# A convolution and a Laplace layer: the pole transform over 128 couples of opposite frequencies, the conjugate rows of the residues exchanged inside the matmul, and the table pieces spaced

## The chip, the cores and the metric

The kernel runs on one NeuronCore of a Trainium2 chip. The metric is the device time of one execution in microseconds (us). The engines are TensorE (PE, with its weight loads shown as PEld), VectorE (DVE), ScalarE (ACT), GpSimd (POOL) and SyncE (SP), which here only issues transfers. Each engine works through its own instructions in order.

## The reference, cut to what matters

Two layers, each added to its input after a group normalization. The first is a circular 3x3 convolution. The second multiplies the 2-D Fourier transform of the image by rational functions of the frequency, given by poles and residues. All is float32, with 16 images of 16 channels of 256 x 256.

```python
def reference(x, w, ty, tx, pole1, pole2, residue):
    x = x + conv3x3_circular(group_norm(x), w)                  # layer 0
    v = group_norm(x)                                           # layer 1
    alpha = fft2(v)
    omega1 = 2j*pi*fftfreq(Ny, dty); omega2 = 2j*pi*fftfreq(Nx, dtx)
    A  = 1.0 / (omega1[:, None, None, None] - pole1[None])      # [256, i, o, 4]
    Bm = 1.0 / (omega2[:, None, None, None] - pole2[None])
    S  = einsum('ikpq,oikp,xikq->oxik', residue, A, Bm)
    r1 = einsum('biox,oxik->bkox', alpha, S)                    # transfer function
    C  = einsum('biox,oikp->bikpx', alpha, A)                   # projections on the poles
    D  = einsum('bikpx,xikq->bikpq', C, Bm)
    r2 = einsum('bikpq,ikpq->bkpq', D, residue)
    x1 = ifft2(r1).real
    x2 = ...  # sum over p, q of r2 * exp(pole1 * ty) * exp(pole2 * tx), real part
    return x + x1 + x2 / (Nx * Ny)
```

For the projections the kernel does not transform the images with A and Bm at every frequency. It transforms A and Bm themselves along the frequency axis, once, into tables of functions of the position: that is the pole transform. For each side there are 16 x 16 x 4 = 1024 complex poles. 1/(i*w - p) at the frequencies w and -w has numerators and denominators in common, which the change uses.

## The kernel before

There are four stages. In the first the convolution runs image by image, in 24 steps an image, and between its steps small pieces of set-up work are issued: statistics of the next image, and generators that build tables for the later stages. The second takes the transforms of the images and the projections, the third sums and mixes with the residues, the fourth transforms back and writes the result. The set-up generators and the loop of the first stage:

```python
    def omega(o, k, d):
        nc.vector.tensor_scalar(o, k, d, 2.0 * PI, ALU.mult, ALU.mult)

    def make_hat(side):                      # pole transform, side 0 = y, 1 = x
        nc.sync.dma_start(out=hatT, in_=a[f"hatT{side}"])
        kcol = sw.tile([P, 2], FP, name="s_kcol", tag="s_kcol")
        nc.sync.dma_start(out=kcol, in_=a["kcol"])
        omega(kcol, kcol, rd[:, side : side + 1])
        n = C * C * 4
        to = ((tabE[:, 1:], tabO[:, :C]), (hB[:, 0], hB[:, 1]))[side]
        for half in range(2):
            pb = sw.tile([P, n // 2, 2], FP, name="s_pb", tag="s_pb")
            nc.sync.dma_start(
                out=pb,
                in_=a[f"pole{side + 1}"][half * 512 : half * 512 + 512].partition_broadcast(P),
            )
            yield
            re = [sw.tile([P, n // 2], FP, name="s_re", tag=f"s_re{h}") for h in range(2)]
            im = [sw.tile([P, n // 2], FP, name="s_im", tag=f"s_im{h}") for h in range(2)]
            dens = [sw.tile([P, n // 2], FP, name="s_den", tag=f"s_den{h}") for h in range(2)]
            pr, pi = pb[:, :, 0], pb[:, :, 1]
            for h in range(2):
                k = kcol[:, h : h + 1]
                nc.scalar.activation(im[h], pi, AF.Identity, bias=k, scale=-1.0)
                nc.scalar.activation(dens[h], pi, AF.Square, bias=k, scale=-1.0)
                if h == 0:
                    nc.gpsimd.tensor_tensor(re[1], pr, pr, ALU.mult)
                nc.gpsimd.tensor_tensor(dens[h], dens[h], re[1], ALU.add)
                yield
            for h in range(2):
                w, r, den = im[h], re[h], dens[h]
                nc.vector.reciprocal(den, den)
                yield

                nc.gpsimd.tensor_tensor(r, pr, den, ALU.mult)
                nc.vector.scalar_tensor_tensor(w, w, -1.0, den, ALU.mult, ALU.mult)
                yield
            yield
            for eo in range(2):
                hv = to[eo].rearrange("p i (m r) -> p i m r", r=2)[:, 8 * half : 8 * half + 8]
                for ri in range(2):
                    ps = psu.tile([P, 512], FP, name="ps_setup", tag="ps_setup")
                    for h in range(2):

                        parts = (((2, re), (1, im)), ((0, im), (1, re)))[ri]
                        for j, (at, src) in enumerate(parts):
                            nc.tensor.matmul(
                                ps,
                                lhsT=hatT[:, h, at, eo],
                                rhs=src[h],
                                start=h == 0 and j == 0,
                                stop=h == 1 and j == 1,
                            )
                        yield
                    nc.scalar.copy(hv[:, :, :, ri], ps.rearrange("p (i m) -> p i m", i=8))

    def make_coef():


    # ... make_coef, make_exps (the exponentials' tables): not touched ...

    def make_c():                            # the residues' matrices
        # ... loads, poles' parts, rc[:, st]: residues, st = 1 the conjugate ...
        for k0 in range(0, C, 2):
            # ... den, num on POOL; yield
            nc.vector.reciprocal(den, den)
            # ... w on POOL: 128 rows x (s = 2, i = 4, m = 8) columns for each of odd, i0 + ii
            yield
            nc.gpsimd.tensor_tensor(num, num, den, ALU.mult)
            yield
            yield
            c4 = sw.tile([P, 4, N], FP, name="s_c", tag="s_pb")
            for i0 in range(0, 4, 2):
                c = c4[:, i0 : i0 + 2]
                ps = psu.tile([P, 2, N], FP, name="ps_setup", tag="ps_setup")
                for ii in range(2):
                    for odd in range(2):
                        nc.tensor.matmul(
                            ps[64 * odd : 64 * odd + 64, ii],
                            lhsT=w[:, odd, i0 + ii].rearrange("p s i m -> p (s i m)"),
                            rhs=num[:, odd],
                            start=True,
                            stop=True,
                        )
                yield
                nc.scalar.copy(c, ps)

                for odd in range(2):
                    rows = slice(64 * odd + 32, 64 * odd + 64)
                    o = c[rows].rearrange("p i (h n) -> p i h n", h=2)
                    s = ps[rows].rearrange("p i (h n) -> p i h n", h=2)
                    for h in range(2):
                        copy = (nc.scalar.copy, nc.vector.tensor_copy)[odd]
                        copy(o[:, :, h, 1:], s[:, :, 1 - h, 1:])
                yield
            nc.sync.dma_start(out=cD[:, :, k0 // 2], in_=c4)

    # ... the loop over the steps of the convolution
    tables = (
        (2, 0, chain(make_hat(0), make_hat(1), make_c())),
        (5, 1, chain(make_exps(0), make_exps(1), make_coef())),
    )
    for g in range(24 * B + 3):
        conv(g)                              # 16 matmuls of 32 x 32 x 512, evictions on ACT
        # ... loads of images, statistics of the next image
        for every, first, gen in tables:
            if g % every == first:
                next(gen, None)              # one piece: up to the generator's next yield
```

A `yield` ends a piece, so one piece of the first chain is issued after every second step of the convolution, and one of the second chain after every fifth. `ps_setup` is a pool with one PSUM buffer, shared by all pieces. In `conv(g)` the tiles have 32 rows and 32 columns, so that sixteen matmuls can stand in the array beside each other; an accumulation takes six steps.

The constants of the pole transform (`hatT`) hold cosines and sines of all 256 frequencies, in two halves of 128, each folded into even and odd positions (`eo`).

Of the kernel before, what the change touches and what calls it, by code (L numbers as in the profile page):

```python
# [9 lines left out]
FP = mybir.dt.float32  # L10
AF = mybir.ActivationFunctionType
ALU = mybir.AluOpType
# [5 lines left out]
C = 16  # L18
N = 256
P = 128  # L20
PI = float(np.pi)
# [3 lines left out]
def conv_then_laplace_kernel(ctx: ExitStack, tc: tile.TileContext, a: dict, out: bass.AP):  # L25
# [15 lines left out]
    nc = tc.nc  # L41
# [3 lines left out]
    dp = ctx.enter_context(tc.tile_pool(name="scratch", bufs=1, space=DRAM))  # L45
# [6 lines left out]
    cols = const("cols", [P, 24])  # L52
# [7 lines left out]
    aD = dp.tile([P, 2 * C, N * B], FP, name="aD", tag="aD")  # L60
    yD = dp.tile([P, 2 * C, 4, 4, 16 * B], FP, name="yD", tag="yD")
    cD = dp.tile([P, 4, 8, N], FP, name="cD", tag="cD")
    eD = [dp.tile([n, P, C, 2, P], FP, name=f"eD{n}", tag=f"eD{n}") for n in (2, 1)]


    def omega(o, k, d):
        nc.vector.tensor_scalar(o, k, d, 2.0 * PI, ALU.mult, ALU.mult)
# [4 lines left out]
    rd = cp.tile([P, 2], FP, name="rd", tag="rd")  # L72
# [24 lines left out]
    p1 = ExitStack()  # L97
    wp = p1.enter_context(tc.tile_pool(name="conv_w", bufs=1))
# [5 lines left out]
    sw = p1.enter_context(tc.tile_pool(name="setup", bufs=1))  # L104
# [241 lines left out]

    def make_hat(side):

        hatT = wp.tile([P, 2, 3, 2, P], FP, name="hatT", tag="hatT")
        nc.sync.dma_start(out=hatT, in_=a[f"hatT{side}"])
        kcol = sw.tile([P, 2], FP, name="s_kcol", tag="s_kcol")
        nc.sync.dma_start(out=kcol, in_=a["kcol"])
        omega(kcol, kcol, rd[:, side : side + 1])
        n = C * C * 4
        to = ((tabE[:, 1:], tabO[:, :C]), (hB[:, 0], hB[:, 1]))[side]
        for half in range(2):  # L360
            pb = sw.tile([P, n // 2, 2], FP, name="s_pb", tag="s_pb")
            nc.sync.dma_start(
                out=pb,
                in_=a[f"pole{side + 1}"][half * 512 : half * 512 + 512].partition_broadcast(P),
            )
            yield
            re = [sw.tile([P, n // 2], FP, name="s_re", tag=f"s_re{h}") for h in range(2)]
            im = [sw.tile([P, n // 2], FP, name="s_im", tag=f"s_im{h}") for h in range(2)]
            dens = [sw.tile([P, n // 2], FP, name="s_den", tag=f"s_den{h}") for h in range(2)]
            pr, pi = pb[:, :, 0], pb[:, :, 1]  # L370
            for h in range(2):
                k = kcol[:, h : h + 1]
                nc.scalar.activation(im[h], pi, AF.Identity, bias=k, scale=-1.0)
                nc.scalar.activation(dens[h], pi, AF.Square, bias=k, scale=-1.0)
                if h == 0:
                    nc.gpsimd.tensor_tensor(re[1], pr, pr, ALU.mult)
                nc.gpsimd.tensor_tensor(dens[h], dens[h], re[1], ALU.add)
                yield
            for h in range(2):
                w, r, den = im[h], re[h], dens[h]  # L380
                nc.vector.reciprocal(den, den)
                yield

                nc.gpsimd.tensor_tensor(r, pr, den, ALU.mult)
                nc.vector.scalar_tensor_tensor(w, w, -1.0, den, ALU.mult, ALU.mult)
                yield
            yield
            for eo in range(2):
                hv = to[eo].rearrange("p i (m r) -> p i m r", r=2)[:, 8 * half : 8 * half + 8]
                for ri in range(2):  # L390
                    ps = psu.tile([P, 512], FP, name="ps_setup", tag="ps_setup")
                    for h in range(2):

                        parts = (((2, re), (1, im)), ((0, im), (1, re)))[ri]
                        for j, (at, src) in enumerate(parts):
                            nc.tensor.matmul(
                                ps,
                                lhsT=hatT[:, h, at, eo],
                                rhs=src[h],
                                start=h == 0 and j == 0,  # L400
                                stop=h == 1 and j == 1,
                            )
                        yield
                    nc.scalar.copy(hv[:, :, :, ri], ps.rearrange("p (i m) -> p i m", i=8))

    def make_coef():

# [67 lines left out]
    def make_c():  # L475
# [4 lines left out]
        om = space[:, 0:N]  # L480
# [3 lines left out]
        z = space[:, 2 * N : 2 * N + 64].rearrange("p (j k) -> p j k", j=4)  # L484
# [30 lines left out]
        for k0 in range(0, C, 2):  # L515

            at = k0 // 2 % 2
# [11 lines left out]
            for odd in range(2):  # L529
                for st in range(2):  # L530
# [10 lines left out]
                        ALU.mult,  # L541
                    )
            yield
            nc.gpsimd.tensor_tensor(num, num, den, ALU.mult)
            yield
            yield
            c4 = sw.tile([P, 4, N], FP, name="s_c", tag="s_pb")
            for i0 in range(0, 4, 2):
                c = c4[:, i0 : i0 + 2]
                ps = psu.tile([P, 2, N], FP, name="ps_setup", tag="ps_setup")  # L550
                for ii in range(2):
                    for odd in range(2):
                        nc.tensor.matmul(
                            ps[64 * odd : 64 * odd + 64, ii],
                            lhsT=w[:, odd, i0 + ii].rearrange("p s i m -> p (s i m)"),
                            rhs=num[:, odd],
                            start=True,
                            stop=True,
                        )
                yield  # L560
                nc.scalar.copy(c, ps)

                for odd in range(2):
                    rows = slice(64 * odd + 32, 64 * odd + 64)
                    o = c[rows].rearrange("p i (h n) -> p i h n", h=2)
                    s = ps[rows].rearrange("p i (h n) -> p i h n", h=2)
                    for h in range(2):
                        copy = (nc.scalar.copy, nc.vector.tensor_copy)[odd]
                        copy(o[:, :, h, 1:], s[:, :, 1 - h, 1:])
                yield  # L570
            nc.sync.dma_start(out=cD[:, :, k0 // 2], in_=c4)

    def chain(*gens):
        for gen in gens:
            yield from gen
# [8 lines left out]
    for b in range(1, B):  # L584
        at_step.setdefault(max(0, 24 * b - 40), []).append((b, x_stats(b)))
    going = []
    tables = (
        (2, 0, chain(make_hat(0), make_hat(1), make_c())),
        (5, 1, chain(make_exps(0), make_exps(1), make_coef())),
    )  # L590
    early = v_stats(0, B - 4, lambda: pst.tile([P, 512], FP, name="ps_stat", tag="ps_stat"))
# [633 lines left out]
def _constants():  # L1225
# [23 lines left out]
        [w * tcos.T[ox], w * tsin.T[ox], -w * tsin.T[ox], tcos.T[o], tsin.T[o]], 1  # L1249
    )  # L1250

    th = 2 * np.pi * (np.outer(j, j) % N) / N
    t = np.stack([np.cos(th), np.sin(th)]).reshape(2, 2, P, N)
    t = np.stack([t[..., :P] + t[..., : P - 1 : -1], t[..., :P] - t[..., : P - 1 : -1]], 3) / 2

    t = np.concatenate([t, -t[:1]]).transpose(2, 1, 0, 3, 4)
    c["hatT0"] = t
    lo, hi = t[..., :64], t[..., :63:-1]
    c["hatT1"] = np.concatenate([lo + hi, lo - hi], -1) / 2
    k = (j + P) % N - P  # L1260
    c["kcol"] = k.reshape(2, P).T
    c["kslot"] = np.concatenate([p, -f_sin])[None]
    c["kmask"] = p[:, None] // 8 == np.arange(C)[None]
    cols = np.zeros((P, 24))
# [48 lines left out]
def _laid_out(x, L0_conv_weight, L1_conv_ty, L1_conv_tx, L1_conv_weights_pole1, L1_conv_weights_pole2, L1_conv_weights_residue):  # L1313
# [26 lines left out]
        pairs(np.asarray(z))  # L1340
        for z in (L1_conv_weights_pole1, L1_conv_weights_pole2, L1_conv_weights_residue)
    )
    g["pole1"], g["pole2"] = p1.reshape(-1, 2), p2.reshape(-1, 2)

    g["res_kq"] = np.repeat(rs.transpose(1, 3, 0, 2, 4).reshape(64, C, 4, 2), 2, 0)

# [28 lines left out]
```

## Time and profile before

| | |
|---|---|
| time before | 2893.25 us, median of 3 runs (2887.61 to 2897.32) |
| span of the profiled execution | 2897.0 us |
| busy: PE, PEld, DVE, ACT, POOL | 92%, 68%, 67%, 53%, 35% |
| first stage (convolution and tables) | 0 to 726 us; first convolution matmul at 29.6 us |
| convolution matmuls (L238) | 12288 instructions, 477.4 us busy |
| pole transform matmuls (L396) | 128 instructions, first at 54.8 us, last at 313.9 us |
| residue matmuls (L553) | 128 instructions, first at 340.9 us, last at 552.6 us |
| chain that ended last | begins at 739 us and ends with the kernel |

One float32 matmul of the program shows as two MATMUL instructions in the profile, so 64 transform matmuls give 128 instructions. A row of the groups reads: line, engine, operation, output <- inputs, shape and count; then the busy time of the group and the mean duration of one instruction in ns; then the time that the engine sat idle just before them and which instruction ended it. Ends of matmuls are modelled, so starts are the better mark. "issue" is a gap for which the profile shows no wait.

### The profile page before, as it was taken

The numbers are of one execution on the slowest core, as the hardware profiler recorded it, in microseconds if no ns is written. First come the engines' busy times: TensorE is split into PE (matmuls) and PEld (weight loads), VectorE is DVE, ScalarE is ACT, GpSimd is POOL, SyncE is SP. The second block draws the span as 40 slices with busy tenths as digits, with TensorE's granted clock in tenths as the row PEclk, the third lists the DMA queues.
The fourth block names the chain that finished last, engine by engine and source line by source line (L and its number), as shares of the span: only waits on it lengthen the run. The fifth ranks groups of instructions, "written<-read, shape, count | busy, mean of one in ns | idle before, by whom it ended". The sixth has DMA issues, their size and how long they took to land.

```text
span 2897.0 us, 92787 instructions
## 1 busy us (share of the span) xinstructions
PE 2667.3 (92%) x39536; PEld 1971.8 (68%) x39536; DVE 1940.5 (67%) x3572; ACT 1536.0 (53%) x3098; POOL 1003.5 (35%) x906
## 2 busy tenths in 40 slices
PE   4878878889799999997899999999969999999998
PEld 2333334346577777775688888888868888888887
DVE  7766698886788888887444444444427666766666
ACT  3556677667466666664345555555524444444443
POOL 2232566420233333333211111111135554555553
PEclk9989998899899999998899999999989999999999
DMA  6555667665566666664466666666679999888995
GB/s 257 203 179 187 212 238 256 229 240 192 182 211 211 233 233 224 227 218 169 150 193 191 191 196 193 193 192 191 190 212 312 285 285 288 285 284 285 290 288 188
DMA packets 477335, 650.63 MB, mean 225 GB/s; under 512 B 49065, under 2 KB 458665, under 8 KB 462969
## 3 DMA queue, kind: packets, MB, share of 16 engines
q1 hardware_dynamic: 472920, 635.37, 67.0%
q8 instruction: 312, 5.11, 0.7%
q10 hardware_dynamic: 3408, 7.34, 0.7%
q0 software_dynamic: 592, 1.97, 0.3%
q14 instruction: 103, 0.84, 0.1%
HBM read 365.09 MB, written 279.45 MB: 222 GB/s over the span
## 4 chain that ended last, share of the span: by engine, by line
PE 56%; DMA 9%; DVE 6%; SPq 2%; POOL 1%; issue 1%; ACT 0%; DVEq 0%; ACTq 0%; POOLq 0%
PE ps_mix L967 15%; PE ps_s L909 8%; PE ps_y L678 8%; PE ps_y L686 8%; DMA yk<-yD 4%; PE ps_x L721 4%; PE ps_p L1148 4%; PE ps_f L1157 3%; PE ps_f L1158 3%; DMA out_y<-ol 3%; DVE r L1166 2%; PE psd L706 1%; DVE ol L1168 1%; DVE ol L1169 1%; SPq L1099 1%; DMA yD<-yt 1%
## 5 line engine op out<-in xcount | busy, mean ns | idle before, releaser
L238 PE MATMUL ps_conv<-xt,wc 32*32 32x512 f32 x12288 | 477.4, 641 | 18.0 <-ACT vt L255 11.2
L967 PEld LDWEIGHTS ps_mix<-abd,sg 128*64 128x64 f32 x8192 | 448.5, 138 | 65.5 <-ACT sg L1027 49.8
L967 PE MATMUL ps_mix<-abd,sg 128*64 128x128 f32 x8192 | 479.4, 276 | 13.4 <-ACT yt L1032 13.4
L1112 POOL TENSOR_TENSOR u<-yk 128x512 f32<-128x512 f32 x256 | 342.2, 1366 | 369.8 <-PE ps_p L1148 241.6
L694 ACT ACTIVATE t<-ps_y,vmr 128x384 f32<-128x384 f32 x512 | 297.7, 582 | 168.4 <-PE ps_y L686 157.0
L238 PEld LDWEIGHTS ps_conv<-xt,wc 32*32 32x32 f32 x12288 | 231.8, 106 | 214.8 <-issue 142.1
L1032 DVE COPY yt<-ps_mix 128x512 f32<-128x512 f32 x128 | 88.6, 692 | 363.8 <-PE ps_mix L967 231.8
L678 PE MATMUL ps_y<-tabE,vq 128*128 128x256 f32 x1024 | 313.1, 387 | 13.9 <-DVE vq L667 12.2
L887 POOL TENSOR_TENSOR w<-v,mcol 128x2048 f32<-128x2048 f32 x33 | 119.3, 3614 | 583.8 <-DVE v L884 580.8
L1157 PE MATMUL ps_f<-pt,inv 128*128 128x256 f32 x1024 | 305.8, 380 | 0.0
L686 PE MATMUL ps_y<-tabO,vq 128*128 128x256 f32 x1024 | 305.7, 380 | 0.0
L1158 PE MATMUL ps_f<-hs,ey 128*128 128x256 f32 x1024 | 305.0, 379 | 0.0
L1032 ACT COPY yt<-ps_mix 128x512 f32<-128x512 f32 x384 | 221.6, 587 | 147.2 <-PE ps_mix L967 95.8
L1148 PEld LDWEIGHTS ps_p<-inv,u 128*128 128x128 f32 x2048 | 265.1, 192 | 49.2 <-issue 24.3
L1148 PE MATMUL ps_p<-inv,u 128*128 128x128 f32 x2048 | 278.1, 279 | 12.6 <-POOL u L1115 12.5
L909 PE MATMUL ps_s<-ct,w 64*32 64x256 f32 x8448 | 260.6, 382 | 27.1 <-DMA ct<-cD 27.1
L1161 DVE TENSOR_TENSOR r<-ps_f,q 128x256 f32<-128x256 f32 x256 | 107.2, 419 | 252.1 <-ACT q L1160 252.1
L255 ACT ACTIVATE vt<-ps_conv,xq 128x512 f32<-128x512 f32 x256 | 167.1, 680 | 194.0 <-PE ps_conv L238 193.0
L1027 ACT COPY sg<-ps_s 128x512 f32<-128x512 f32 x248 | 159.9, 646 | 199.7 <-PE ps_s L909 199.5
L678 PEld LDWEIGHTS ps_y<-tabE,vq 128*128 128x128 f32 x1024 | 189.5, 190 | 90.3 <-ACT q L734 50.3
L1160 ACT COPY q<-ps_f 128x256 f32<-128x256 f32 x256 | 95.4, 373 | 290.8 <-PE ps_f L1158 290.8
L909 PEld LDWEIGHTS ps_s<-ct,w 64*32 64x32 f32 x8448 | 158.4, 107 | 92.3 <-POOL abd L1011 27.9
(214 smaller groups left out, 4165.0 us busy)
## 6 DMA issues: line engine op xcount, KB each, us to landing
xt<-in_x SPq DMA_DIRECT2D x32, 2322.0 KB, 9.6
abd<-aD SPq DMA_DIRECT2D x512, 128.0 KB, 3.3
yD<-yt SPq DMA_DIRECT2D x512, 128.0 KB, 2.6
vl<-vD SPq DMA_DIRECT2D x256, 256.0 KB, 3.9
out_y<-ol SPq DMA_DIRECT2D x128, 512.0 KB, 9.8
yk<-yD SPq DMA_DIRECT2D x63, 1024.0 KB, 8.6
s<-vD SPq DMA_DIRECT2D x244, 256.0 KB, 5.9
aD<-spec SPq DMA_DIRECT2D x15, 4096.0 KB, 13.3
```

What stands on the lines that cost most here:

```text
L238: nc.tensor.matmul(acc[r][32 * c : 32 * c + 32], lhsT=ready[b][0][rows, phase, tap], rhs=halves[b][u // 2][rows, q : q + 5 : 4, 2 - tap : ...
L255: nc.scalar.activation(vt[:, r % 2], acc[r], AF.Identity, bias=ready[b][1], **by_sums)
L678: nc.tensor.matmul(ps[:, 0:N], lhsT=vf[:, xo, 0, j], rhs=tabE[:, 0 : i + 2 : i + 1], start=True, stop=False, skip_group_check=True,)
L686: nc.tensor.matmul(ps[:, P : P + N], lhsT=vf[:, xo, 1, j], rhs=tabO[:, i : C + 1 : C - i], start=False, stop=True, skip_group_check=True,)
L694: nc.scalar.activation(t[:, xo, j].rearrange("p l n -> p (l n)"), ps[:, 0:384], AF.Copy, scale=vmr[:, 0, b0 + j, i : i + 1],)
L909: nc.tensor.matmul(ps[odd][32 * iq : 32 * iq + 32, ro], lhsT=w[rows, iq, kk, ro], rhs=ct[rows, iq, kk], start=True, stop=True,)
L967: nc.tensor.matmul(ps[64 * t : 64 * t + 64, j], lhsT=sg[:, f : f + 2].rearrange("p f m -> p (f m)"), rhs=abd[jq][:, :, 2 * t + cc, 2 * jj ...
L1032: (nc.vector.tensor_copy if m == 3 else nc.scalar.copy)(o, src)
L1112: nc.gpsimd.tensor_tensor(u[:, :, j].rearrange("p b (c n) -> p c b n", c=8), in0, in1, o)
L1148: nc.tensor.matmul(ps[:, at], lhsT=u[:, n], rhs=tab, start=True, stop=True)
L1157: nc.tensor.matmul(ps[:, e], lhsT=tab, rhs=pt[:, e], start=True, stop=False)
L1158: nc.tensor.matmul(ps[:, e], lhsT=ey[:, e], rhs=hs, start=False, stop=True)
```

## The change

Three things are changed, all in the set-up generators of the first stage.

The pole transform is taken over 128 couples (w, -w) instead of 256 frequencies. The sum and the difference of 1/(iw - p) and 1/(-iw - p) are rational in w squared: with m = |p|^2, sq = re^2 - im^2 and nb = -2 re im, the common denominator is g = (w^2 + sq)^2 + nb^2, and the four real quantities needed come from re, im, m, sq and nb. These five depend on the pole alone. A new generator, `make_poles`, computes them once for all poles, 16 values in each of 128 partitions, writes them to a scratch tensor in DRAM (`hD`), and `make_hat` loads them spread over all partitions. The couple in partition 0 is made of the frequencies 0 and 128; its values go into `hD` as two further rows (qr, qi) and are loaded over row 0.

For the residues, the conjugate rows (`st` = 1) need the two halves of the frequencies exchanged. Before, copies out of PSUM did that; now the matmul of those rows reads its moving operand with the halves reversed, so the matmuls have 32 columns instead of 64, and only entries 0 and 128 are exchanged by copies.

Further `yield`s are put between the pieces: after the copy out of the setup bank, ahead of the product of `num`, and after the loads.

```diff
+    hD = dp.tile([7, 2, C * C * 4], FP, name="hD", tag="hD")
 ...
+    def make_poles():
+        pz = sw.tile([P, 64, 16], FP, name="s_pz", tag="s_pb")
+        re, im, m, sq, nb, qr, qi, r2, t = (pz[:, j] for j in range(9))
+        nc.sync.dma_start(out=pz[:, 0:2], in_=a["poles"])
+        yield
+        yield
+        # ... thirteen-odd small operations on DVE: m, sq, nb, qr, qi, -im
+        yield
+        nc.sync.dma_start(
+            out=hD.rearrange("c s (p e) -> p (c s) e", e=8),
+            in_=pz[:, 0:7].rearrange("p c (s e) -> p (c s) e", e=8),
+        )
+        yield
+        yield
 ...
     def make_hat(side):
 ...
+        n = C * C * 2
         for half in range(2):
 ...         # the body shown above is replaced
+            pr, npi, m, sq, nb, g, b2 = tiles
+            at = slice(half * n, half * n + n)
+            for j in range(5):
+                nc.sync.dma_start(out=tiles[j], in_=hD[j, side, at].partition_broadcast(P))
+            yield
+            yield
+            if half == 0:
+                omega(om1, om1, rd[:, side : side + 1])
+                nc.vector.tensor_tensor(om2, om1, om1, ALU.mult)
+                # ... hatT[:, 1] is scaled by om1 (1 in row 0)
+            yield
+            nc.scalar.activation(g, sq, AF.Square, bias=om2)
+            nc.scalar.activation(b2, nb, AF.Square)
+            yield
+            nc.gpsimd.tensor_tensor(g, g, b2, ALU.add)
+            yield
+            nc.vector.reciprocal(g, g)
+            yield
+            for z in (pr, npi, nb):
+                nc.gpsimd.tensor_tensor(z, z, g, ALU.mult)
+            yield
+            nc.vector.scalar_tensor_tensor(sq, sq, om2, g, ALU.add, ALU.mult)
+            yield
+            nc.vector.scalar_tensor_tensor(pr, m, om2, pr, ALU.add, ALU.mult)
+            nc.vector.scalar_tensor_tensor(npi, m, om2, npi, ALU.subtract, ALU.mult)
+            for j, z in ((5, sq), (6, nb)):
+                nc.sync.dma_start(out=z[0:1], in_=hD[j, side, at].unsqueeze(0))
+            yield
             yield
             for eo in range(2):
 ...
+                for ri, parts in enumerate(((pr, sq), (npi, nb))):
                     ps = psu.tile([P, 512], FP, name="ps_setup", tag="ps_setup")
+                    for j, src in enumerate(parts):
+                        nc.tensor.matmul(
+                            ps, lhsT=hatT[:, j, eo], rhs=src, start=j == 0, stop=j == 1
+                        )
+                    yield
                     nc.scalar.copy(hv[:, :, :, ri], ps.rearrange("p (i m) -> p i m", i=8))
+                    yield
 ...
     def make_c():
 ...
             yield
+            yield
             nc.gpsimd.tensor_tensor(num, num, den, ALU.mult)
 ...
                 for ii in range(2):
                     for odd in range(2):
-                        nc.tensor.matmul(
-                            ps[64 * odd : 64 * odd + 64, ii],
-                            lhsT=w[:, odd, i0 + ii].rearrange("p s i m -> p (s i m)"),
-                            rhs=num[:, odd], start=True, stop=True,
-                        )
+                        halves_of = num[:, odd].rearrange("p (h n) -> p h n", h=2)
+                        for st in range(2):
+                            at = 64 * odd + 32 * st
+                            nc.tensor.matmul(
+                                ps[at : at + 32, ii].rearrange("p (h n) -> p h n", h=2),
+                                lhsT=w[:, odd, i0 + ii, st].rearrange("p i m -> p (i m)"),
+                                rhs=halves_of[:, ::-1] if st else halves_of,
+                                start=True, stop=True,
+                            )
                 yield
                 nc.scalar.copy(c, ps)
                 for odd in range(2):
                     rows = slice(64 * odd + 32, 64 * odd + 64)
-                    # ... two copies of 32 x 254, on ACT for odd = 0 and DVE for odd = 1
+                    nc.scalar.copy(c[rows, :, 0:N:P], ps[rows, :, P::-P])
+                yield
                 yield
 ...
-        (2, 0, chain(make_hat(0), make_hat(1), make_c())),
+        (2, 0, chain(make_poles(), make_hat(0), make_hat(1), make_c())),
```

The constants shrink with it: `hatT` has 2 x 2 x 128 columns instead of 2 x 3 x 2 x 128 a side, and the poles reach the kernel as real and imaginary parts, 16 in each partition.

## The prediction

> **What bounds the kernel now.** I first asked for the chain that ended last. It runs through the second, third and fourth stage, but it leads back only to 739 us, so it says nothing of the convolution stage, in which everything that the change touches is issued. That stage has to end before the next can read its stored images, so what shortens it shortens the kernel. I then asked for the busy time by stretches of it: time, then PE, PEld, DVE, ACT and POOL busy with instruction counts, the granted clock, the DMA share and GB/s.
>
> ```profile
> 28.00:305.00 277.00, 226.51 (x4039) 93.07 (x4040) 190.06 (x283) 149.44 (x325) 89.85 (x73) 0.91 0.52 185
> 305.00:560.00 255.00, 209.79 (x4787) 101.94 (x4790) 219.20 (x349) 177.34 (x407) 148.93 (x159) 0.90 0.68 238
> 560.00:600.00 40.00, 35.67 (x918) 19.35 (x894) 29.52 (x52) 29.28 (x68) 9.97 (x10) 0.96 0.79 270
> 600.00:650.00 50.00, 39.14 (x926) 19.63 (x922) 43.35 (x87) 34.74 (x78) 8.79 (x8) 0.90 0.68 246
> 650.00:700.00 50.00, 47.07 (x1328) 28.50 (x1333) 38.07 (x87) 35.92 (x89) 3.05 (x3) 0.97 0.59 204
> 700.00:726.00 26.00, 23.51 (x703) 18.17 (x676) 13.33 (x14) 22.32 (x59) 0.00 (x0) 0.99 0.50 168
> ```
>
> The first stretch holds the pole transforms, the second the residues' matrices, the others neither. A convolution step is 16 matmuls, 32 instructions in the trace. The same query for the convolution's own matmuls gives 3888 in the first stretch, 4613 in the second, 3143 in the three from 560 to 700 together, 703 in the last. So a step takes 277/(3888/32) = 2.28 us beside the pole transforms, 255/(4613/32) = 1.77 us beside the residues, 140/(3143/32) = 1.43 us beside neither, and 1.18 us at the very end, where even the statistics of the next image are gone. The table work thus costs 0.85 us a step in the first part and 0.34 us in the second, some 100 + 50 = 150 us in all. No other engine is full: DVE has 69% in the first stretch and 86% in the second.
>
> The groups on PE in the stage and PE's waits (total, times, longest) show where it goes:
>
> ```profile
> L396 PE MATMUL ps_setup<-s_re,hatT 128*128 128x512 f32 x64 | 39.5, 703 | 8.4 <-ACT tabE L404 5.2 <-ACT hB L404 3.2
> L396 PE MATMUL ps_setup<-s_im,hatT 128*128 128x512 f32 x64 | 39.1, 696 | 19.0 <-ACT hB L404 10.6 <-ACT tabO L404 4.7 <-ACT tabE L404 3.7
> L553 PE MATMUL ps_setup<-s_num,s_w 128*64 128x256 f32 x128 | 22.3, 479 | 38.3 <-DVE s_c L569 21.3 <-POOL s_num L544 16.9
> ```
>
> The transforms hold PE for 78.6 us and make it wait for 27.4; the residues hold it for 22.3 and make it wait for 38.3. These 167 us are close to the 150 from the step times. So I take PE, with what it waits for in its order, as the bound. A piece of the timeline (start, duration) shows one cycle:
>
> ```profile
> 218.35 1.12 PE L396 MATMUL ps_setup<-s_im,hatT 128*128 128x512 f32 x2 [3.15 <-ACT hB L404]
> 219.31 1.02 PE L396 MATMUL ps_setup<-s_re,hatT 128*128 128x512 f32 x2
> 220.26 2.35 PE L238 MATMUL ps_conv<-xt,wc 32*32 32x512 f32 x64
> 222.54 1.12 PE L396 MATMUL ps_setup<-s_im,hatT 128*128 128x512 f32 x2
> 223.50 1.02 PE L396 MATMUL ps_setup<-s_re,hatT 128*128 128x512 f32 x2
> 224.45 2.35 PE L238 MATMUL ps_conv<-xt,wc 32*32 32x512 f32 x64
> 227.74 0.58 ACT L404 COPY hB<-ps_setup 128x512 f32<-128x512 f32 x1
> 228.38 1.12 PE L396 MATMUL ps_setup<-s_re,hatT 128*128 128x512 f32 x2 [1.58 <-ACT hB L404]
> ```
>
> Two pieces of two matmuls (1.91 us each, from start to the convolution's next start), four convolution steps, and a stop of 1.58 us: the copy out of the only setup bank is issued in the same turn as the next matmul into it. From 218.35 to 228.38 it is 10.03 us for four steps, 2.51 us a step.
>
> **What the skill says.** The Trainium skill, TensorEngine Tiling, section Key Properties: a change of tiling mode drains TensorE. The convolution works in 32x32 tiles, the transforms in the full array, so every piece pays a drain twice; the trace shows weight loads idle for 0.84 us ahead of a piece and 0.76 us after it. Half as many pieces means half as many drains. PSUM - Partial Sum Buffer, section Engine vs sequencer instructions: the other engines' queues are strict FIFO and matmuls keep program order. The stop in the timeline agrees: convolution matmuls that need nothing of the copy stand behind the one that does. TensorE: Matmul & The Clock Gate, Part 1: an idle PE gets a slower clock. The trace agrees: 0.91 and 0.90 in the stretches with table waits, 0.99 in the last. So a wait removed may also raise the clock; I count little for it.
>
> **The change part by part.**
>
> (1) Transform over 128 couples. Per (eo, ri) there are two matmuls instead of four, so 32 instead of 64, or 64 of the 128 instructions go. By the two L396 rows that is half of 78.6, 39 us of PE, nearly all on the path.
>
> (2) The copy gets a turn of its own. Every matmul of the transforms then starts two steps after the copy that frees the bank. This aims at the 27.4 us of waits. Cross-check of (1) and (2) on the cycle: one piece and four steps between 1.18 and 1.43 us make 6.6 to 7.6 us instead of 10.03; sixteen such cycles save 39 to 55 us. The sum 39 + 27 = 66 is above it, since a PE that is let go early meets the next wait. I take 50.
>
> (3) Residues. Two full copies stay at 16 x 0.57 us; the four exchange copies per bank (32 on ACT at 0.36, 32 on DVE at 0.42) become two tiny ACT copies for entries 0 and 128. DVE loses 12.3 us, ACT at most 10.0 less 32 x 0.2 (the 128x1 ACT operations' row) = 4 us. The bank is freed by ACT alone, and an extra turn stands behind the copies and another ahead of the num product. The 21.3 us of waits for s_c should go and half of the 16.9 for s_num. The matmuls are now 32 columns wide, sixteen instructions a bank in four column groups instead of eight in two: four rounds in either case, so the same time. The projections' 128*32 matmuls speak for that: sixteen of 128 columns took 0.66 us together. Of about 30 us I count 20, as DVE is at 86% here.
>
> (4) Less on the other engines. Per half, one reciprocal (3.34 us) instead of two, three DVE products (0.80) instead of two; DVE loses 4 x (3.34 - 0.8) = 10 us, with (3) some 22, less about 4 for the new small operations on 16 columns and the scaled matrix. ACT loses 8 x 0.8 = 6 us. POOL keeps four products a half, 4 x 1.4, against five. DVE's 551 us in 28 to 752 fall to about 533. This makes room; I count 5 us.
>
> (5) What it adds. A first part: one load, thirteen DVE operations on 128x16 (0.2 us each), a store to DRAM. Then five broadcast loads of 256 KB a half in place of one of 512 KB, 3 MB more in all; at the 200 GB/s of the stage 15 us of transfer, beside other work, with the DMA at 0.5 to 0.7. The store is in pieces of 32 B; DMA: Bandwidth & Descriptors, Specifications, gives 512 B as the least for full rate; no row of this trace measures it. It occurs once, and the loads stand behind it in the same queue. I count 3 us lost for it and for waits on these loads.
>
> (6) Spacing. The chain has one turn per two steps. Turns before: 4 x 16 + 68 = 132, so 264 steps. After: 5 + 4 x 18 + (4 + 8 x 11) = 169, so 338 of the 387 steps. It still ends inside the stage, so nothing is left for an unhidden tail.
>
> Sum: 50 + 20 + 5 - 3 = 72 us. The other way, by rates: the first 154 steps hold 64 at about 1.8 us and 90 at 1.65 (264 us), then 184 at 1.62 (298), then 46 at 1.43 (66); with the 28 us at the start the stage ends at 656 instead of 726, 70 us less. I predict 2893 - 73 = 2820 us.
>
> **Rivals.** First, DVE takes over: it needs 533 us, and with the pauses of the FIFO a share of over 88% was never held across a long stretch. Then the stage can't fall below about 635 to 640, and in the residues' part, already at 86%, waits only move from ACT to DVE. The gain would be 45 us, 2848. For it speaks the stretch 600 to 650: no tables at all, DVE at 87%, and yet 1.75 us a step. Second, waits for data: ACT now takes its first square six steps after issuing the loads, behind the store and five broadcasts. The four old loads landed after 4.2 to 19.9 us, and POOL waited 88.1 us for three of them without harm. If ACT waits, the convolution's evictions stand behind it; 10 us a half gives 2855 to 2865. Third, the waits were all of it and the clock rises as well: steps of 1.45 us throughout put the end near 600 us, 2770.
>
> **Range and chances.** 2820, from 2782 to 2862: the low end is most of the third rival, the high end DVE and load waits together. 2% is 57.9 us, a time under 2835; the central value passes it by 15 us only, and DVE's rival falls short. Faster 0.65, within 2% 0.31, slower 0.04; a slowdown would take loads that block the queue for over 100 us.
>
> **What would show it.** Right: 64 transform instructions with about 39 us busy; PE's waits for tabE, tabO, hB and s_c near nil; steps of about 1.75 us in the first part and 1.6 in the second; first matmuls of the second stage near 665 us; later stages unchanged. Wrong: ACT waiting for hD's loads, SyncE held by that store, DVE over 90% with PE waiting for it, or residue matmuls well above 22 us.

## The result, and the profile after

The changed kernel takes 2820.74 us (median of 4 runs, 2815.98 to 2822.70) against 2894.41 us of the kernel before in the same comparison: a ratio of 0.9746, 95% interval 0.9725 to 0.9768, or 73.7 us less. The prediction was 2820 us.

The second stage's first matmul starts at 657.0 us in the profiled execution instead of 735.7, 79 us earlier, and the rest of the kernel is nearly as long as before (2166 us from 648 on, 2171 from 726 on). So 79 of the 83 us between the two profiled executions (spans 2814.2 and 2897.0 us) lie in the first stage. Its stretches, with the columns of before (busy time of PE, PEld, DVE, ACT and POOL with counts, clock, DMA share, GB/s); the first ends with the pole transforms, the second with the residues:

```profile
28.00:298.00 270.00, 231.09 (x5034) 109.79 (x5049) 221.16 (x367) 177.90 (x397) 104.15 (x77) 0.94 0.75 247
298.00:590.00 292.00, 245.97 (x6160) 122.57 (x6158) 264.25 (x422) 215.81 (x505) 165.36 (x171) 0.94 0.74 256
590.00:648.00 58.00, 53.00 (x1544) 35.46 (x1524) 35.37 (x72) 44.05 (x115) 0.00 (x0) 1.00 0.52 180
```

In these the convolution has 4928, 5856 and 1538 of its instructions, 32 a step. So a step takes 1.75 us beside the pole transforms (2.28 before), 1.60 beside the residues (1.77 before), 1.21 after both. VectorE (the third busy column) has 82% of the first stretch, where it had 69%, and 90% of the second. It holds this for long in parts of the second:

```profile
298.00:398.00 100.00, 92.20 (x2289) 46.58 (x2286) 96.01 (x154) 79.12 (x186) 60.48 (x63) 0.95 0.78 269
398.00:498.00 100.00, 85.41 (x2224) 42.97 (x2224) 89.99 (x138) 78.21 (x183) 66.75 (x68) 0.98 0.78 278
```

The groups of set-up matmuls on PE (busy time, mean ns, idle time before them and what ended it):

```profile
L438 PE MATMUL ps_setup<-s_re,hatT 128*128 128x512 f32 x32 | 19.9, 706 | 11.1 <-DVE s_re L427 4.5 <-ACT hB L442 3.7 <-ACT tabE L442 3.0
L438 PE MATMUL ps_setup<-s_im,hatT 128*128 128x512 f32 x32 | 18.1, 651 | 0.0
L597 PE MATMUL ps_setup<-s_num,s_w 128*32 128x256 f32 x256 | 17.2, 385 | 0.1
```

The transforms hold PE for 38.0 us instead of 78.6 and wait 6.7 us for copies instead of 27.4, and 4.5 for VectorE's last product (s_re). The residues' matmuls wait for nothing, where they waited 38.3. The other large groups on PE, the convolution and an image's statistics, first two lines before, last two after:

```profile
L238 PE MATMUL ps_conv<-xt,wc 32*32 32x512 f32 x12288 | 477.4, 641 | 18.0 <-ACT vt L255 11.2 <-issue 6.7
L167 PE MATMUL ps_stat<-xq,g 128*128 128x1 f32 x64 | 12.9, 270 | 39.8 <-DVE xq L163 27.8 <-DVE xq L177 11.9
L239 PE MATMUL ps_conv<-xt,wc 32*32 32x512 f32 x12288 | 466.2, 623 | 26.7 <-issue 21.8 <-ACT vt L256 4.7
L168 PE MATMUL ps_stat<-xq,g 128*128 128x1 f32 x64 | 13.3, 277 | 51.8 <-DVE xq L164 39.7 <-DVE xq L178 12.1
```

So by PE's list the edits took away 100 us of matmuls and waits, and the convolution's own matmuls are 11 us shorter (granted clock 0.94 in 28 to 648 us, before 0.92 in 28 to 726). But 28 us came back as stops: 19 ahead of the statistics (12 of them in the lines shown), all for VectorE, and 9 in the convolution, where the time for which the profile shows no wait (issue) has grown by 15. The cycle of a transform in the timeline, PE's rows and ScalarE's copies (start, duration):

```profile
277.68 0.61 ACT L442 COPY hB<-ps_setup 128x512 f32<-128x512 f32 x1
278.34 1.13 PE L438 MATMUL ps_setup<-s_re,hatT 128*128 128x512 f32 x2 [1.47 <-ACT hB L442]
279.30 1.02 PE L438 MATMUL ps_setup<-s_im,hatT 128*128 128x512 f32 x2
280.25 4.49 PE L239 MATMUL ps_conv<-xt,wc 32*32 32x512 f32 x128
283.64 0.71 ACT L442 COPY hB<-ps_setup 128x512 f32<-128x512 f32 x1
284.67 1.13 PE L438 MATMUL ps_setup<-s_re,hatT 128*128 128x512 f32 x2
```

From 278.34 to 284.67 it is one piece of 1.91 us and four steps in 6.33 us; in the prediction's cycle of before, four steps took 10.03. The second copy, at 283.64, falls under the convolution's matmuls and stops nobody.

### The profile page after: what moved, and what is told of

Same layout as the page of the kernel before. It is cut to its first block, busy times and chain, and to the rows that moved or that the text cites. A ratio compares the mean times of both kernels' runs of the same rounds, so it can differ in the third digit from the quotient of the medians.

```text
span 2814.2 us, 92940 instructions
## 1 busy us (share of the span) xinstructions
PE 2615.9 (93%) x39600; PEld 1958.8 (70%) x39600; DVE 1929.7 (69%) x3562; ACT 1523.1 (54%) x3090; POOL 1011.0 (36%) x902
## 4 chain that ended last, share of the span: by engine, by line
PE 57%; DMA 9%; DVE 7%; SPq 2%; POOL 1%; issue 1%; ACT 0%; DVEq 0%; ACTq 0%; POOLq 0%
PE ps_mix L1007 16%; PE ps_s L949 9%; PE ps_y L718 8%; PE ps_y L726 8%; DMA yk<-yD 4%; PE ps_x L761 4%; PE ps_p L1188 4%; DMA out_y<-ol 3%; PE ps_f L1197 3%; PE ps_f L1198 3%; DVE r L1206 2%; PE psd L746 1%; DVE ol L1208 1%; DVE ol L1209 1%; SPq L1139 1%; PE ps_h L1172 1%
## 5 line engine op out<-in xcount | busy, mean ns | idle before, releaser
L239 PE MATMUL ps_conv<-xt,wc 32*32 32x512 f32 x12288 | 466.2, 623 | 26.7 <-issue 21.8
L718 PE MATMUL ps_y<-tabE,vq 128*128 128x256 f32 x1024 | 313.5, 388 | 13.6 <-DVE vq L707 11.9
L1188 PE MATMUL ps_p<-inv,u 128*128 128x128 f32 x2048 | 278.1, 279 | 12.2 <-POOL u L1155 11.9
L949 PE MATMUL ps_s<-ct,w 64*32 64x256 f32 x8448 | 262.2, 382 | 28.0 <-DMA ct<-cD 27.4
## 6 DMA issues: line engine op xcount, KB each, us to landing
xt<-in_x SPq DMA_DIRECT2D x32, 2322.0 KB, 11.2
```

Of the source, the lines that this page charges most:

```text
L239: nc.tensor.matmul(acc[r][32 * c : 32 * c + 32], lhsT=ready[b][0][rows, phase, tap], rhs=halves[b][u // 2][rows, q : q + 5 : 4, 2 - tap : ...
L718: nc.tensor.matmul(ps[:, 0:N], lhsT=vf[:, xo, 0, j], rhs=tabE[:, 0 : i + 2 : i + 1], start=True, stop=False, skip_group_check=True,)
L949: nc.tensor.matmul(ps[odd][32 * iq : 32 * iq + 32, ro], lhsT=w[rows, iq, kk, ro], rhs=ct[rows, iq, kk], start=True, stop=True,)
L1188: nc.tensor.matmul(ps[:, at], lhsT=u[:, n], rhs=tab, start=True, stop=True)
```

## The experiments

The theory is the prediction's: in the first stage PE, with what it waits for in its order, is the bound, so matmuls removed and waits removed count nearly in full. The rival is that VectorE takes over. The pattern to read is which edit moves the time by how much, alone and together. Ratios are to the kernel before in the same comparison.

| run | edit | time, us | ratio, 95% interval |
|---|---|---|---|
| e1_spacing | before + further turns | 2861.85 | 0.9888 (0.9872 to 0.9905) |
| e2_couples | before + couples | 2884.01 | 0.9967 (0.9953 to 0.998) |
| e3_residues | before + exchange in the matmul, with its turns | 2861.43 | 0.9891 (0.9876 to 0.9906) |
| e4_no_spacing | changed kernel - further turns | 2848.87 | 0.9848 (0.9833 to 0.9863) |
| e5_twice | changed kernel, transform matmuls twice | 2840.85 | 0.982 (0.9801 to 0.9839) |
| e6_more_dve | changed kernel + 40 us of VectorE | 2856.27 | 0.9871 (0.9855 to 0.9887) |
| e7_late_stats | changed kernel, statistics later | 2808.02 | 0.9699 (0.9683 to 0.9715) |
| e8_couples_shift | e2, chain from step 8 | 2878.86 | 0.9939 (0.9917 to 0.9961) |
| e9_after_shift | changed kernel, chain from step 8 | 2833.19 | 0.9783 (0.9762 to 0.9805) |
| e10_couples_turn | e2 + turn for the copy | 2857.64 | 0.9875 (0.9848 to 0.9903) |
| e11_copies_act | before, exchange copies on ACT only | 2872.82 | 0.992 (0.9894 to 0.9946) |
| e12_lead | e7, image statistics further apart | 2811.56 | 0.9699 (0.968 to 0.9718) |

### e1_spacing: the turns alone

```diff
                     nc.scalar.copy(hv[:, :, :, ri], ps.rearrange("p (i m) -> p i m", i=8))
+                    yield
 ...
             yield
+            yield
             nc.gpsimd.tensor_tensor(num, num, den, ALU.mult)
 ...
                         copy(o[:, :, h, 1:], s[:, :, 1 - h, 1:])
                 yield
+                yield
```

> The kernel before with nothing but the further turns of the change: one after the copy out of the setup bank in the pole transforms, one ahead of the num product and one after the copies of the residues (chain of 172 turns, 344 steps). Theory (PE and what it waits for in its order is the bound): the 27.4 us of waits for tabE, tabO and hB and most of the 38.3 us before the residue matmuls vanish from PE's list, the 78.6 us of transform matmuls stay, and the time falls by 30 to 45 us, to 2848 to 2863. Rival (VectorE is the bound): the waits move to the statistics and evictions, and the time falls by less than 10 us, to over 2883.

Measured: 2861.85 us, 31 less, inside the theory's range. Not one instruction of work is removed; PE's waits for the copies of the transforms fall from 27.4 to 9.2 us and those ahead of the residue matmuls from 38.3 to 19.1, while the wait ahead of the second small matmul of an image's statistics (xq L177) rises from 11.9 to 19.4. The rival, as far as it speaks of the kernel before, falls.

### e2_couples: half the transform matmuls, no turn

```diff
     changed kernel, with make_c() of before and without
-                    yield          (behind the copy of the transforms)
```

> The transform over couples alone (first part, hD, half of the matmuls), without a turn for the copy, and the residues as before. Theory: half of 78.6 us of PE goes, 39 us, the waits for the copies stay near 27 us, so 2850 to 2862. Rival (VectorE is the bound): only VectorE's 10 us less count, 2880 or above.

Measured: 2884.01 us, 9 less. The theory's number fails: 39 us of matmul were to go. PE's groups in this run:

```profile
L591 PE MATMUL ps_setup<-s_num,s_w 128*64 128x256 f32 x128 | 24.6, 519 | 35.8 <-DVE s_c L607 31.1 <-POOL s_num L582 4.7
L438 PE MATMUL ps_setup<-s_re,hatT 128*128 128x512 f32 x32 | 23.7, 832 | 28.7 <-ACT hB L442 11.9 <-ACT tabE L442 10.3 <-DVE s_re L427 3.4
L438 PE MATMUL ps_setup<-s_im,hatT 128*128 128x512 f32 x32 | 23.0, 811 | 0.0
```

The 64 instructions take 46.7 us, not 39: a piece now has a copy ahead of it each time, and the mean is 832 and 811 ns against 703 and 696 before (granted clock 0.87 in 128 to 228 us, 0.90 before). The waits for the copies stay, 25 us. Ahead of the residue matmuls PE waits 35.8 us, before 38.3: the wait for s_c has grown by 10 and that for s_num fallen by 12. What has grown is the wait for VectorE ahead of the second small matmul of an image's statistics, to 29.3 us from 11.9:

```profile
L168 PE MATMUL ps_stat<-xq,g 128*128 128x1 f32 x64 | 13.5, 280 | 59.8 <-DVE xq L164 30.6 <-DVE xq L178 29.3
```

So of the 32 us of matmul that PE was spared, 20 came back as idle time ahead of the statistics (59.8 us against 39.8). The longest of these waits, 10.7 us, ends at 145.6 us, just after VectorE has worked through the transforms' three products (140.5 to 144.3 us).

### e3_residues: the exchange, with its turns

```diff
     kernel before, with make_c() of the changed kernel
```

> The residues alone: the exchange in the matmul and the further turns in that part; the pole transforms as before. Theory: 15 to 25 us less, 2868 to 2878, with the waits for s_c gone and the residue matmuls at about 17 us of PE. Rival: the waits only move, within 8 us of before.

Measured: 2861.43 us, 32 less; the theory's range was 15 to 25, so the edit is worth more than the prediction counted for it. PE's waits ahead of the residue matmuls, 38.3 us before, are gone, and these matmuls take 18.0 us instead of 22.3. With VectorE freed of its copies, the stretches beside the residues run as follows (columns as above; two lines of before, then e3):

```profile
328.00:428.00 100.00, 79.42 (x1860) 38.87 (x1841) 89.58 (x140) 69.76 (x161) 66.59 (x75) 0.92 0.66 231
428.00:528.00 100.00, 80.75 (x1773) 38.32 (x1759) 85.30 (x127) 66.75 (x155) 66.59 (x70) 0.86 0.69 239
328.00:428.00 100.00, 85.18 (x2175) 40.87 (x2162) 94.24 (x144) 77.19 (x182) 75.52 (x75) 0.98 0.75 262
428.00:528.00 100.00, 91.58 (x2370) 45.29 (x2353) 96.14 (x143) 81.22 (x190) 64.27 (x60) 0.98 0.82 288
```

VectorE is at 94% and 96%, where the same 100 us had 90% and 85% before.

### e4_no_spacing: the changed kernel without its turns

The edit is that of e1, backwards.

> The changed kernel without its further turns (the copy and the next matmul in one turn again, residues with two turns a bank and none ahead of the product). Theory: matmuls and copies saved are kept, but PE waits again for tabE, tabO and hB, some 27 us, and for s_num, so 20 to 35 us slower than the changed kernel, 2841 to 2856. Rival (the matmuls saved are the whole gain and the turns do nothing): within 8 us of the changed kernel, under 2829.

Measured: 2848.87 us, 28 more than the changed kernel, inside the theory's range. The waits come back:

```profile
PE ps_setup L438 <- ACT hB L442: 11.9, 5, 3.7
...
PE ps_setup L595 <- ACT s_c L606: 10.4, 7, 3.1
PE ps_setup L438 <- ACT tabE L442: 10.3, 3, 3.6
...
PE ps_setup L438 <- ACT tabO L442: 3.1, 1, 3.1
```

Against e2, which has neither these turns nor the exchange and a chain of the same length, e4 is 35 us faster: the exchange gives that much without any further turn.

### e5_twice: the matmul time put back

```diff
-                    for j, src in enumerate(parts):
+                    for j, src in 2 * list(enumerate(parts)):
```

> The changed kernel with every pair of transform matmuls issued twice into the same bank, so that PE has the 64 matmuls of before again, in 16 larger pieces; all else, the turns too, as in the changed kernel. Theory (the matmul time of the transforms lies on the path): 28 to 39 us slower than the changed kernel, 2849 to 2860. Rival (VectorE is the bound, PE has slack in these turns): less than 12 us slower, under 2833.

Measured: 2840.85 us, 20 more than the changed kernel, between the two. The doubled matmuls add 64 instructions and 33 us (the transforms' matmuls take 71.2 us instead of 38.0), so some 60% of it shows in the time. PE's stops did not shrink to make up for the rest: in both kernels they come to 113 us up to the end of the stage. The convolution's own matmuls are 7 us shorter (459.0 us against 466.2); what is left is open.

### e6_more_dve: 40 us more on VectorE

```diff
             nc.vector.reciprocal(g, g)
+            more = sw.tile([P, N], FP, name="s_more", tag="s_more")
+            for h in range(2):
+                nc.vector.reciprocal(more, g[:, h * N : h * N + N])
     (and the same behind reciprocal(den, den), with den[:, h])
```

> The changed kernel with 12 further reciprocals of 512 elements on VectorE (each in two halves, into a scratch tile that nobody reads), one behind each reciprocal of the chain: some 40 us more of VectorE in the stage, none of PE. If PE is the bound and VectorE has room: 5 to 15 us slower than the changed kernel, 2826 to 2836. If VectorE is the bound now: 30 to 40 us slower, 2850 to 2861.

Measured: 2856.27 us, 36 more than the changed kernel, for 24 reciprocals that take 42 us. This decides for the rival: most of what VectorE has more to do in the chain is time of the kernel. The convolution's own matmuls take 476.9 us instead of 466.2, and PE feels VectorE where it asks for the statistics' small results: its wait for the aggregate of an image (39.7 us in the changed kernel, of which 25.0 is the start) becomes

```profile
PE ps_stat L168 <- DVE xq L164: 52.2, 8, 24.3
```

### e8_couples_shift and e9_after_shift: does the place of the pieces matter?

```diff
-            if g % every == first:
+            if g % every == first and (every == 5 or g >= 8):
```

> The couples alone (as e2_couples), their chain begun at step 8 instead of 2, so that its 129 turns end where the 132 of the kernel before end and the residues' pieces meet the same steps of the images as before. In e2 the transforms' part was some 27 us shorter by its starts, but the residues' part then took 250 us instead of 239, with 31.1 us of waits for s_c against 21.3. If the place of the pieces in the image's steps is what gave the gain back: 2864 to 2874. If the gain is given back for any place, because VectorE is behind: within 5 us of e2, 2879 to 2889.

> The changed kernel with the same shift of its first chain to step 8, a control of how much the mere place of the pieces weighs once they have turns of their own. If place weighs little: within 5 us of the changed kernel, 2816 to 2826. If it weighs as much as 10 us or more, differences of that size between the other variants say nothing of their edits.

Measured: e8 2878.86 us, 5 less than e2 with intervals that just overlap, at the edge of "given back for any place"; its waits for s_c are still 29.3 us. (The chain of before begins at step 0 and not 2, so the shift is one of 8 steps, and the residues' pieces come two steps later than in the kernel before.) The wait ahead of the second small matmul of the statistics, 29.3 us in e2, does depend on place: it is 27.0 in e4, where VectorE has no exchange copies to make, and 13.3 in e8, where nothing but the place differs. But e8's transforms wait 12.1 us for s_re, where e2's waited 3.4. The control, e9, is 12 us slower than the changed kernel, outside its range: PE's wait for s_re rises from 4.5 to 13.5 us there. So the place of the pieces in an image's 24 steps weighed 12 us here, and a difference of that size between two variants with chains of different length is not evidence for their edits. What follows rests on the larger ones.

### e10_couples_turn: couples and turn, residues as before

```diff
     e2, with again
+                    yield          (behind the copy of the transforms)
```

> The couples with the copy's own turn, residues as before. The three edits then stand as a chain: before, couples (e2), couples with turn (this), changed kernel. If the turn is worth what e4 says (28 us) also without the exchange: 2852 to 2860, and the exchange is the remaining 32 to 38 us. If VectorE's s_c copies hold everything up: over 2868.

Measured: 2857.64 us, inside the first range: 36 less than before and 26 less than e2. The step from here to the changed kernel, the exchange with its turns, is 37 us. Taken in the other order, from e3 to the changed kernel, couples and turn are worth 41 us. In this run the exchange copies still hold up both engines; the tile's list of who waited for it:

```profile
  DVE s_c L608: 32.1, 5
  PE ps_setup L592: 24.9, 7
```

VectorE stood 32.1 us for ScalarE's copies, ahead of 13 us of its own copies.

### e11_copies_act: VectorE out of the exchange, nothing else

```diff
-                        copy = (nc.scalar.copy, nc.vector.tensor_copy)[odd]
-                        copy(o[:, :, h, 1:], s[:, :, 1 - h, 1:])
+                        nc.scalar.copy(o[:, :, h, 1:], s[:, :, 1 - h, 1:])
```

> The kernel before with one edit: the two exchange copies of the odd rows go to ScalarE as well, so that VectorE neither spends 12.3 us on them nor stands 19.2 us behind ScalarE's copies, while ScalarE gets about 12 us more, and no turn and no matmul is changed. If VectorE's part in s_c is what the exchange in the matmul saves: 15 to 30 us faster than before, 2863 to 2878. If the bank's late release is what costs (TensorE waits for the last copy, which now comes later): within 8 us of before or slower.

Measured: 2872.82 us, 20.5 less than before, inside the first range, though ScalarE has 12 us more work and PE still waits for the bank:

```profile
PE ps_setup L553 <- ACT s_c L568: 11.9, 5, 3.6
```

With the wait for s_num, 9.2 us, PE now waits 21.1 us ahead of the residue matmuls instead of 38.3: what VectorE no longer does reaches PE as shorter waits there. The chain is as long as before, so place plays no part. More than half of what the exchange gives is had by taking VectorE's copies, and its standing ahead of them, out of that place.

### e7_late_stats and e12_lead: a version that beats both

```diff
-        if g > 24 * (B - 4) + 8 and g % 3 == 0:
+        if g > 24 * (B - 4) + 56 and g % 3 == 0:          (e7)
-        yield 24, lambda: nc.vector.bn_aggr(q[:, 0:2], st)
+        yield 25, lambda: nc.vector.bn_aggr(q[:, 0:2], st) (e12, besides; 14 -> 13, 12 -> 11, 5 -> 4, 3 -> 2)
```

> The changed kernel with the statistics of the first twelve images begun 48 steps later (step 345 instead of 297). In the changed kernel the chain of tables has grown from 264 to 338 steps and now meets them; TensorE waited 10.4 us at once for VectorE there and the steps from 500 to 575 us are the slowest of the second part. Theory (that meeting costs time): 8 to 18 us faster than the changed kernel, 2803 to 2813. Rival (VectorE's work is only moved): within 4 us of it.

> e7 (statistics of the first twelve images begun 48 steps later) with the pieces of each image's own statistics set further apart: the aggregate one step earlier, the second and third small matmul, the root and the bias one step later each, so that VectorE has a step more before TensorE asks for its result. In e7 TensorE still waited some 32 us for these small results, without the first image's 24.9. If VectorE's lateness at these points lies on the path: 5 to 12 us faster than e7, 2796 to 2803. If VectorE's amount of work is the limit: within 4 us of e7.

Measured: e7 2808.02 us, 13 less than the changed kernel, and its interval lies wholly below. The stretch of the residues shows it; the first line is e7's, to be held against the 298 to 590 line of the changed kernel:

```profile
298.00:590.00 292.00, 257.83 (x6394) 127.47 (x6394) 263.17 (x427) 219.47 (x520) 167.43 (x171) 0.94 0.76 263
```

VectorE is as busy as it was there, 263 us against 264, but PE has 258 us instead of 246: work that nobody needed yet is moved behind the tables. e12 gives nothing more (2811.56, the interval around the same ratio): PE's waits for two of the small results fall from 10.8 and 8.5 us to 6.5 and 2.0, its stops in the convolution rise by as much, from 28.5 to 38.7, and the time stays. Earlier small results alone gain nothing. That fits the rival, that VectorE's amount of work is the limit, an amount which this run did not change.

## Why the prediction was right, and where its terms were not

**The place of the gain** was right: the first stage alone, 79 us in the profile. The second stage was to start its matmuls near 665 us and started at 657.

**The steps' rates** were right: 1.75 and 1.6 us were predicted for the two parts, 1.75 and 1.60 were measured. The cycle of the transform was to fall from 10.03 to between 6.6 and 7.6 us. The one shown, 6.33 us, is the shortest; the twelve of the changed kernel (between the four banks of a half, in four halves) last 7.5 us on average, those of before 12.4, so that the 10.03 was below the average too.

**(1) and (2), couples and the copy's turn, 50 us:** mis-sized. The two, with their share of (4) and (5), give 36 in e10 and 41 on top of the exchange. The turn is sound: 26 on top of e2; together with the residues' two further turns 31 in e1 and 28 in e4. The couples are not 39: 9 alone, 14 when shifted, 20 by e5. The step that failed is "39 us of PE, nearly all on the path". In e2 the matmuls shrank by 32 us and PE's idle time ahead of the statistics grew by 20; in e5, 33 us of matmuls put back cost 20.

**(3) the exchange, with its turns, 20 us:** mis-sized the other way, 32 alone and 37 on top of the others. Of the 38.3 us of waits in PE's list the prediction counted about 30 and cut that to 20 for VectorE's load; all of them went. It also overlooked, besides VectorE's 12.3 us of copies, the time that VectorE stood for ScalarE's copy ahead of them, which the waits of before show:

```profile
DVE s_c L569 <- ACT s_c L569: 19.2, 5, 5.1
```

e11 takes both away and gives 20.5. The rest, the bank's earlier release, the turns and the matmuls, was not separated. The matmuls were predicted to cost the same; 256 narrow instructions take 17.2 us, 1.07 a bank, against 22.3 for 128 wide ones before. But the wide ones differ from stretch to stretch. Before, in two stretches with two banks each (behind the length of 25 us stands PE's busy time; the third figure from the right is the granted clock):

```profile
400.00:425.00 25.00, 2.12 (x16) 1.06 (x16) 1.54 (x4) 1.19 (x3) 0.98 0.62 222
475.00:500.00 25.00, 3.06 (x16) 1.26 (x16) 1.54 (x4) 2.40 (x6) 0.86 0.65 234
```

That is 1.06 us a bank at 0.98 and 1.53 at 0.86, so near full clock wide and narrow cost the same, as predicted.

**(4) VectorE's relief, 5 us:** over the stretch that had 551 us of VectorE, 538 are left against a predicted 533, so 13 us went and not 18; but by e6 such relief counts for the most part, not as mere room. It can't be added to the terms above, since part of it is in them.

**(5) additions, 3 us:** not settled. ScalarE shows no wait for a load from hD; the loads landed in 5.4 to 7.8 us at the median, the store in 2.8. SyncE stood 28 us at that store, once, without a follow-up on PE's list. So the second rival falls as it was put. But VectorE waits longer for the images than before (first line):

```profile
DVE xst L155 <- DMA xt<-in_x: 6.0, 4, 2.9
DVE xst L156 <- DMA xt<-in_x: 22.4, 7, 7.2
```

Of the 22.4 us, 11.7 fall before 220 us, in the part in which hD is loaded (45.6 to 233.4 us), where it was 0.5 before, and the images' loads land after 11.2 us at the median instead of 9.6. Whether hD's loads delay them was not tested.

**(6) spacing:** the chain ends inside the stage, as counted, but it then meets the statistics of the first twelve images, which the prediction did not see. e7 shows 13 us for it.

**The first rival, VectorE takes over,** was half right and belonged in the main line: in the residues' part VectorE is at 90% of 292 us, and 42 us more on it cost 36. Its number, 2848, is 27 us too slow: the stage ended near 648 us. The prediction's remark that over 88% is never held is wrong; the kernel before held 89.6% for 100 us, and 96% was held for 100 us after. Of **the third rival**, a higher clock, a small part came true: 11 us in the convolution's own matmuls.

The place of the gain and where it comes from were understood; that the sum came out right to 1 us was luck: (1) and (2) were counted 9 to 14 us too high, (3) 12 to 17 too low. Up to 12 us of any single term may be place (e9); what an edit is worth free of place stays open below that size.

## What to carry to other kernels

When two engines are both near full, an engine's busy time is a poor price for an edit: ask which engine's queue stands at which wait, and add the time that an engine stands for another's result to the time that it works. Put the release of a single buffer and its next use into different turns; here that gave 26 us on top of e2, and 28 to 31 with the residues' further turns, without removing any work, at the price of a longer chain. After a chain of background work has been lengthened, look for what it now meets, and measure a mere shift of the chain before reading small differences.

## What the runs showed that was not expected

The same full-array matmuls took 703 and 696 ns on average before, 832 and 811 in e2, 706 and 651 after. In e2, with a copy to wait for ahead of nearly every piece, they run at a lower granted clock; the traces show stops and clock together, and that the one causes the other was not tested. A store to DRAM in pieces of 32 B, 56 KB in all, landed in 2.8 us.
